# A selective scan with its last product on GpSimd and its step input in PSUM, and attention values on the whole TensorE array with their denominators as extra rows

## The chip, the cores and the metric

The kernel runs on one core of a Trainium2 chip. A core has TensorE (PE, matmuls into the accumulator memory PSUM), VectorE (DVE), ScalarE (ACT) and GpSimd (POOL), which work on the on-chip memory SBUF[...], and SyncE (SP), which issues DMA transfers. [...] Each engine runs its own instructions in order and waits for others by semaphores. The metric is the device time of one execution, in microseconds (us): the median of three runs is 20,853.4, the lowest 20,836.71, the highest 20,863.03.

## What is computed

The program is a chain of four layers on an input of 8 images, 64 channels (C), 64 x 64 pixels (L = 4096 positions). What matters here, from the reference:

```python
# layer 0: state-space scan, in four directions, 128 channels, 16 states
def step(h, inp):
    u_t, dt_t, B_t, C_t = inp
    h = h * jnp.exp(dt_t[..., None] * A) + dt_t[..., None] * B_t[:, :, None, :] * u_t[..., None]
    return (h, jnp.einsum('bkcn,bkn->bkc', h, C_t))
...
return jnp.moveaxis(ys, 0, -1) + D[None, :, :, None] * xs
...
# layer 1: position attention, q and k with 16 channels
energy_s = jnp.einsum('bon,bom->bnm', q, k)
att_s = jax.nn.softmax(energy_s, axis=-1)
out_s = jnp.einsum('bcn,bmn->bcm', v, att_s).reshape(b, c, h, w)
...
# layer 3: position attention, 64 channels
attention = jnp.einsum('nci,ncj->nij', xc, xb)
att = jax.nn.softmax(attention, axis=-1)
x_o = jnp.einsum('ncj,nij->nci', xd, att).reshape(n, c, h, w)
return alpha[0] * x_o + x
```

Before the scan stand a layer norm, a projection to 128 channels and a 3 x 3 depthwise convolution; after it a norm, a gate and a projection. Layer 0 ends with a gated convolution, layer 1 also has a channel attention, and layer 2 takes two training steps of a small network before it applies it. The change touches none of these.

## The kernel before

Three stages follow each other: `scan_layer` (to about 10,980 us of the span), `gate_and_attention` (the gated convolution, then the first attention, to about 14,900), and `modifier_and_attention` (the training steps, then the second attention from about 18,100 on).

**The scan.** For each of 8 images there are 16 chunks: four directions (in the order 0, 2, 1, 3) of four chunks of 1024 positions (CH). Each chunk runs over 16 states n, so there are 2048 inner steps. Channels lie on the 128 partitions, positions along the free dimension. One step:

- SP loads the rows n of B and of C, broadcast over all partitions, into the 1 MB tile `t` (L261; four buffers).
- ACT forms `a` = exp(dt A) (L263; two buffers).
- DVE multiplies `t[:,0]` by `du` in place (L264), scans `h` = a h + t0 along the chunk (L266) and multiplies `t[:,1]` by `h` in place (L271). The scan starts from the state column that the same n left in the chunk before.
- POOL copies the last column of `h` into the `state` tile (L270).
- PE adds `t[:,1]` into the PSUM tile `yps` by a matmul with the identity (L273).

After the 16 states a skip matmul (L279) adds D u, and `yps` goes into `y`: by an ACT copy for the first direction (L285), by a DVE add for the others (L287). `yps` has two buffers of two banks each; four banks are left for everything else.

`project` prepares the next chunk: matmul and ACT copy to `xd`, its rows B and C to memory (L233), a second matmul and ACT for `dt` (L236, L237), three ACT functions into `e` (L240 to L242), DVE's softplus sum `dt` (L243, two SBUF inputs) and POOL's `du` = dt u (L245). Directions 1 and 3 read u, and write y, across rows (`ordered`). At the end of an image `before(b+1)` (norm, projection, convolution L204) is issued before the last chunk's scan, and `after(b)` behind it: norm, then for each of eight blocks of 512 a matmul `zps`, ACT's gate, a DVE product (L304), the matmul `ops`, a DVE sum (L307). The order on each engine is set by the scheduler of the framework, from the order of the program and the buffers of the pools.

**The attentions** (`Attention.run`). For each image q, k and v are formed; v holds 32 blocks of 128 keys by 64 channels. The queries go in 8 blocks of 512. For each block 16 pairs of key blocks run through: scores on row tiles of the array (L426), an exp of 128 x 1024 on ACT (L431), sums of the exps on DVE (L436, L438), and values (L446). The values use two column tiles of the array: the even key block of a pair goes to partitions 0 to 63 of the PSUM tile `av`, the odd one to 64 to 127. The loop takes two pairs at a time (a group) and issues the scores of a group ahead of the values of the group before. Two groups after the end of a block comes `divide`: a matmul of the exp sums with a tile of ones (`sumps`, L454) spreads the denominators, DVE takes the reciprocal (L456), multiplies (L458) and records whether the denominators are in range (L462). Two groups later `finish` adds even and odd halves by a matmul with `fold` (the identity twice, one above the other). In the first attention it is added to the channel attention's matmul in the same PSUM tile and copied out by ACT (L744, L745, L747); in the second DVE adds the input (L1129, L1131).

Of the kernel before, what the change touches and what calls it, by code (L numbers as in the profile page):

```python
# [9 lines left out]
F32 = mybir.dt.float32  # L10
# [32 lines left out]
class Common:  # L43


    def __init__(self, ctx, tc):
        self.tc, self.nc = tc, tc.nc
        nc = self.nc
        self.open(ctx, "const")
        self.ident = self.tile([128, 128], "ident")  # L50
        make_identity(nc, self.ident)
        self.ones = self.tile([128, C], "ones")
        nc.vector.memset(self.ones, 1.0)
        self.all_ones = self.tile([128, 128], "all_ones")
        nc.vector.memset(self.all_ones, 1.0)

        self.fold = self.tile([128, C], "fold")
        nc.vector.tensor_tensor(self.fold, self.ident[:, :C], self.ident[:, C:], ALU.add)
# [75 lines left out]
def scan_layer(cm, x_in, w, xh):  # L134

    tc, nc = cm.tc, cm.nc
    with ExitStack() as ctx:
# [81 lines left out]
        def project(u, k, c):  # L219

            uo = ordered(u, k, c)
            half = BK // S
            xd = work.tile([R + 2 * N, CH], F32, name="xd", tag="xd")
            dt = work.tile([DI, CH], F32, name="dt", tag="dt")
            for i in range(CH // BK):
                ps = psum.tile([128, BK], F32, name="dps", tag="mm")
                nc.tensor.matmul(
                    ps[: R + 2 * N].rearrange("p (a b) -> p a b", b=S), wx[:, k, :],
                    uo[:, i * half : (i + 1) * half, :], start=True, stop=True,
                )  # L230
# [12 lines left out]
            nc.vector.scalar_tensor_tensor(dt, dt, 0.0, e, ALU.max, ALU.add)  # L243
            du = work.tile([DI, CH], F32, name="du", tag="du")
            nc.gpsimd.tensor_tensor(  # L245
                du.rearrange("p (a b) -> p a b", b=S), dt.rearrange("p (a b) -> p a b", b=S),
                uo, ALU.mult,
            )
            return dt, du, bc

        def scan(u, y, k, c, first, prep, state):
# [7 lines left out]
            for n in range(N):  # L259
                t = bcp.tile([DI, 2, CH], F32, name="t", tag="bc")  # L260
                nc.sync.dma_start(t, bcr[n].unsqueeze(0).broadcast_to([DI, 2, CH]))  # L261
                a = work.tile([DI, CH], F32, name="a", tag="a")
                nc.scalar.activation(a, dt, AF.Exp, scale=amat[:, k, n : n + 1])  # L263
                nc.vector.tensor_tensor(t[:, 0, :], t[:, 0, :], du, ALU.mult)  # L264
                h = work.tile([DI, CH], F32, name="h", tag="h")
                nc.vector.tensor_tensor_scan(  # L266
                    h[:, flip], a[:, flip], t[:, 0, flip],
                    0.0 if state is None else state[:, n : n + 1], ALU.mult, ALU.add,
                )
                nc.gpsimd.tensor_copy(new[:, n : n + 1], h[:, last : last + 1])  # L270
                nc.vector.tensor_tensor(t[:, 1, :], t[:, 1, :], h, ALU.mult)  # L271
                for i in range(CH // BK):
                    nc.tensor.matmul(  # L273
                        ps[:, bass.ts(i, BK)], cm.ident, t[:, 1, bass.ts(i, BK)],
# [83 lines left out]
class Attention:  # L358
# [3 lines left out]

    LOW, HIGH, VMAX = 1e-20, 1e26, 1e10

    def __init__(self, cm, ctx, name, d, qw, qb, kw, kb, vw, vb, gain, work, psum, sc, av):
# [19 lines left out]
        cm.load_t(work, psum, self.wv[:C, :], vw)  # L388
        nc.sync.dma_start(self.wv[C : C + 1, :], _row(vb))
        nc.vector.tensor_scalar(self.wv, self.wv, g, None, ALU.mult)  # L390

        self.lim = cm.tile([1, NB, NBK, 2], name + "_lim")
        self.vmax = cm.tile([128, NB], name + "_vmax")

    def run(self, b, xa, finish):
# [2 lines left out]
        cm, nc, d = self.cm, self.cm.nc, self.d  # L398
        q = self.pool.tile([128, L], F32, name="q", tag="q")
        k = self.pool.tile([128, L], F32, name="k", tag="k")  # L400
        v = self.pool.tile([128, TQ, C], F32, name="v", tag="v", bufs=2)
        for j in range(NBK):
            blk = bass.ts(j, BK)
            for t, wt in ((q, self.wq), (k, self.wk)):
# [8 lines left out]
            nc.vector.tensor_copy(v[:, 4 * j : 4 * j + 4, :], ps[:, :, :C])  # L413
        nc.vector.tensor_reduce(
            self.vmax[:, b : b + 1], v, AX.XY, ALU.max, apply_absolute_value=True
        )
        pairs = [(i, g) for i in range(NBK) for g in range(TQ // 2)]
        avs, sums, firsts = {}, {}, {}
        in_range = self.pool.tile([1, BK], F32, name="in_range", tag="in_range", bufs=1)

        def scores(i, g):
# [7 lines left out]
                )  # L429
            ex = self.exps.tile([128, 2, BK], F32, name="ex", tag="ex")  # L430
            nc.scalar.activation(ex, sc, AF.Exp)  # L431
            if g == 0:
                firsts[i] = ex
            elif g == 1:
                sums[i] = self.work.tile([128, 2, BK], F32, name="sum", tag="sum")
                nc.vector.tensor_tensor(sums[i], firsts[i], ex, ALU.add)  # L436
            else:
                nc.vector.tensor_tensor(sums[i], sums[i], ex, ALU.add)  # L438
            return ex

        def values(i, g, ex):
# [2 lines left out]
            av = avs[i]  # L444
            for e in range(2):
                nc.tensor.matmul(  # L446
                    av[e * C : (e + 1) * C, :], v[:, 2 * g + e, :], ex[:, e, :],
                    start=(g == 0), stop=(g == TQ // 2 - 1),
                )

        def divide(i):
            ps = self.psum.tile([128, BK], F32, name="sumps", tag="mm")
            for e in range(2):
                nc.tensor.matmul(ps, cm.all_ones, sums[i][:, e, :], start=(e == 0), stop=(e == 1))  # L454
            rr = self.work.tile([128, BK], F32, name="rr", tag="rr")
            nc.vector.reciprocal(rr, ps)  # L456
            o = self.work.tile([128, BK], F32, name="o", tag="o")
            nc.vector.tensor_tensor(o, rr, avs[i], ALU.mult)  # L458
            for e, (op, v0) in enumerate(
                ((ALU.is_ge, 1.0 / self.HIGH), (ALU.is_le, 1.0 / self.LOW))  # L460
            ):
                nc.vector.tensor_scalar(  # L462
                    in_range, rr[0:1, :], v0, None, op, ALU.min,
                    accum_out=self.lim[0:1, b, i, e : e + 1],
                )
            return o

        ahead, done = [], {}
        groups = [pairs[p : p + 2] for p in range(0, len(pairs), 2)]
        per = TQ // 4
        for n in range(len(groups) + 5):
            now = [(i, g, scores(i, g)) for i, g in groups[n]] if n < len(groups) else []
            for one in ahead:
                values(*one)
            ahead = now
            if n % per == 2 and n > per:
                done[n // per - 1] = divide(n // per - 1)  # L480
            if n % per == 4 and n > per:
                finish(n // per - 1, done.pop(n // per - 1))

    def out_of_range(self):

# [120 lines left out]
def gate_and_attention(cm, xh, w, a, x1, mixes, x2):  # L606

    tc, nc = cm.tc, cm.nc
    with ExitStack() as ctx:
# [56 lines left out]
        for b in range(NB):  # L666
# [416 lines left out]
def modifier_and_attention(cm, x2, w, a, x3, mixes, out):  # L1083
# [3 lines left out]
    with ExitStack() as ctx:  # L1087
# [25 lines left out]
        for b in range(NB):  # L1113
# [64 lines left out]
```

## Time and profile before

| what | value |
|---|---|
| median of three runs | 20,853.4 us |
| profiled execution | 20,863.03 us |
| its span | 20,861.2 us |
| mean granted TensorE clock | 0.772 of full speed |
| ACT, exp of the scan, L263 | 2,348.9 us in 2048 |
| POOL, state copy L270 / du L245 | 2,819.9 us in 2048 / 546.4 us in 128 |
| PE, identity matmuls L273 | 5,439.9 us in 8192 records |
| t loads | 2048 of 1,024 KB, median 5.3 us from issue to landing |
| DVE L456, reciprocal of 128 x 512 | mean 3.358 us |

The page gives for each group of instructions the busy time, the mean of one in ns, and the idle time of the engine ahead of it with what ended it. Line numbers are those of the kernel before. An fp32 matmul leaves two records, so the 2048 steps with two matmuls each give 8192. A chunk of the scan takes 76.6 us in the mean (twelve chunks from 1694.96 to 2614.26 us). DVE's longest single wait in the scan is 73.66 us at the end of an image, for `e`, which stands behind the convolution of the next image.

### The profile page before, as it was taken

The page shows a single profiled execution, that of the slowest core. Times are in us where ns is not written, and L with a number is a line of the kernel's source. Part 1 is how long each engine was busy: PE and PEld are TensorE (multiplying, and loading weights), DVE is VectorE, ACT ScalarE, POOL GpSimd, SP SyncE. Part 2 cuts the span into 40 slices and gives each one's busy share as a digit, 9 for nine tenths or more (in the row PEclk, how much of TensorE's full clock was granted, in tenths as well). Part 3 has the DMA queues.
Part 4 walks back from the last instruction along what each step waited for, and adds up shares of the span by engine and source line. Part 5 has one row for each costly group of instructions (what it writes and reads, how often), then busy time and mean ns, then how long its engine had stood idle before and what let it go on. Part 6 is the DMA issues. An engine that isn't in the chain of part 4 may idle for free. (4 is left out here: it accounts for less than half of the span.)

```text
span 20861.2 us, 120440 instructions
## 1 busy us (share of the span) xinstructions
PE 16934.2 (81%) x40899; PEld 5722.3 (27%) x40899; DVE 15083.2 (72%) x11926; ACT 7129.5 (34%) x7767; POOL 3525.7 (17%) x2316
## 2 busy tenths in 40 slices
PE   6676676766766767667668999999989989999999
PEld 2122222221211222222212222222234526333333
DVE  7989979899799798998993444444454726656656
ACT  3333333333333333433332223222313415333333
POOL 2332323323323232232230000000000000000000
PEclk8888787887888878878876777777765756788889
DMA  4646656566466565664660000000020100100000
GB/s 160 218 172 218 218 170 221 180 209 218 166 225 216 172 221 179 209 219 167 224 216 13 7 7 7 7 7 7 5 46 16 27 18 11 24 12 7 10 7 6
DMA packets 599802, 2315.54 MB, mean 111 GB/s; under 512 B 47480, under 2 KB 47752, under 8 KB 592520
## 3 DMA queue, kind: packets, MB, share of 16 engines
q1 hardware_dynamic: 599176, 2307.69, 33.2%
q8 instruction: 333, 5.46, 0.1%
q14 instruction: 293, 2.40, 0.0%
HBM read 2248.54 MB, written 58.98 MB: 111 GB/s over the span
## 5 line engine op out<-in xcount | busy, mean ns | idle before, releaser
L273 PE MATMUL yps<-t,ident 128*128 128x512 f32 x8192 | 5439.9, 801 | 3026.3 <-DVE t L271 2954.8
L263 ACT ACTIVATE a<-dt,amat 128x1024 f32<-128x1024 f32 x2048 | 2348.9, 1148 | 5972.5 <-DVE h L266 5970.5
L270 POOL COPY state<-h 128x1 f32<-128x1 f32 x2048 | 2819.9, 1378 | 6562.7 <-DVE h L266 6557.7
L266 DVE TENSOR_TENSOR_SCAN h<-a,state,t 128x1024 f32<-128x1024 f32 x1536 | 3612.0, 2353 | 12.6 <-ACT a L263 6.3
L273 PEld LDWEIGHTS yps<-t,ident 128*128 128x128 f32 x8192 | 1746.9, 235 | 6731.2 <-DVE t L271 4906.8
L431 ACT ACTIVATE ex<-sc 128x1024 f32<-128x1024 f32 x2048 | 1988.8, 1021 | 2518.8 <-PE sc L426 2518.8
L264 DVE TENSOR_TENSOR t<-t,du 128x1024 f32<-128x1024 f32 x2048 | 2706.5, 1323 | 45.6 <-DMA t<-bc 24.7
L438 DVE TENSOR_TENSOR sum<-sum,ex 128x1024 f32<-128x1024 f32 x1792 | 2184.6, 1219 | 661.2 <-ACT ex L431 570.9
L271 DVE TENSOR_TENSOR t<-t,h 128x1024 f32<-128x1024 f32 x2048 | 2480.8, 1213 | 1.9
L446 PE MATMUL av<-ex,v 128*64 128x512 f32 x8192 | 2009.2, 612 | 0.0
L426 PE MATMUL sc<-q,k 16*128 16x512 f32 (+1 forms) x8192 | 1799.0, 644 | 0.0
L639 PE MATMUL cvps<-pad,fw 64*64 64x512 f32 (+2 forms) x1728 | 1307.6, 959 | 56.1 <-DVE pad L682 56.1
L266 DVE TENSOR_TENSOR_SCAN h<-a,t 128x1024 f32<-128x1024 f32 x512 | 1166.2, 2280 | 3.6 <-ACT a L263 0.7
L426 PEld LDWEIGHTS sc<-q,k 16*128 16x128 f32 (+1 forms) x8192 | 595.3, 188 | 1055.3 <-ACT ex L431 607.7
L446 PEld LDWEIGHTS av<-ex,v 128*64 128x64 f32 x8192 | 503.3, 137 | 1363.1 <-issue 1348.3
L896 PE MATMUL yps<-a,w2T 128*64 128x512 f32 x640 | 575.6, 999 | 192.5 <-ACT a L889 192.4
L245 POOL TENSOR_TENSOR du<-dt,u 128x1024 f32<-128x1024 f32 x128 | 546.4, 4269 | 1038.1 <-DVE dt L243 1036.6
L660 DVE TENSOR_TENSOR gt<-cvps,dbl 64x512 f32<-64x512 f32 x64 | 43.7, 683 | 929.8 <-PE cvps L639 929.8
L704 POOL TENSOR_TENSOR gt<-gt,pad 64x512 f32<-64x512 f32 x64 | 75.2, 1175 | 3728.4 <-ACT gt L703 3590.8
L639 PEld LDWEIGHTS cvps<-pad,fw 64*64 64x64 f32 x1728 | 373.6, 226 | 990.2 <-issue 920.7
L243 DVE SCALAR_TENSOR_TENSOR dt<-dt,e 128x1024 f32<-128x1024 f32 x128 | 155.4, 1214 | 656.9 <-ACT e L242 656.8
L911 DVE BATCH_NORM_STATS2 yst<-yps 64x6 f32<-64x512 f32 x128 | 88.5, 691 | 697.3 <-PE yps L898 697.3
(321 smaller groups left out, 15027.4 us busy)
## 6 DMA issues: line engine op xcount, KB each, us to landing
t<-bc SPq DMA_DIRECT2D x2048, 1024.0 KB, 5.3
x<-x SPq DMA_DIRECT2D x80, 1024.0 KB, 7.4
bc<-xd SPq DMA_DIRECT2D x128, 128.0 KB, 3.4
xn<-in_x_dram SPq DMA_DIRECT2D x8, 1024.0 KB, 7.8
xr<-in_x_dram SPq DMA_DIRECT2D x64, 128.0 KB, 2.9
xh<-xr SPq DMA_DIRECT2D x64, 128.0 KB, 2.2
xt<-xh SPq DMA_DIRECT2D x8, 1024.0 KB, 9.6
x<-xa SPq DMA_DIRECT2D x8, 1024.0 KB, 6.8
```

The costliest lines, as they stand in the source:

```text
L263: nc.scalar.activation(a, dt, AF.Exp, scale=amat[:, k, n : n + 1])
L264: nc.vector.tensor_tensor(t[:, 0, :], t[:, 0, :], du, ALU.mult)
L266: nc.vector.tensor_tensor_scan(h[:, flip], a[:, flip], t[:, 0, flip], 0.0 if state is None else state[:, n : n + 1], ALU.mult, ALU.add,)
L270: nc.gpsimd.tensor_copy(new[:, n : n + 1], h[:, last : last + 1])
L271: nc.vector.tensor_tensor(t[:, 1, :], t[:, 1, :], h, ALU.mult)
L273: nc.tensor.matmul(ps[:, bass.ts(i, BK)], cm.ident, t[:, 1, bass.ts(i, BK)], start=(n == 0), stop=False,)
L426: nc.tensor.matmul(sc[:, e, :], k[rows, bass.ts(j, 128)], q[rows, bass.ts(i, BK)], start=True, stop=True,)
L431: nc.scalar.activation(ex, sc, AF.Exp)
L438: nc.vector.tensor_tensor(sums[i], sums[i], ex, ALU.add)
L446: nc.tensor.matmul(av[e * C : (e + 1) * C, :], v[:, 2 * g + e, :], ex[:, e, :], start=(g == 0), stop=(g == TQ // 2 - 1),)
L639: nc.tensor.matmul(ps, fw[:, i, t, :], pads[i][:, r0 + dy : r0 + nr + dy, dx : dx + n], start=(t == 0), stop=(t == 8),)
L896: nc.tensor.matmul(ps[:C], self.w2T, a, start=True, stop=not residual)
```

## The change

In the scan:

- `du` is formed by DVE into a PSUM tile (one buffer, two banks), not by POOL into SBUF.
- The product of B with `du` goes to a PSUM tile of its own, `z` (tag bdu, one buffer, two banks), and the scan reads it there; `t[:,0]` is left as loaded.
- The state column is copied by ACT, and the product of C with `h` is taken by POOL.
- `a` and `h` have three buffers, not two. `yps` has one, not two, and the pool for everything else two banks, not four; with them all eight banks are taken.

In the attentions:

- v is 128 wide: 64 channels of values and 64 columns of ones, in two tiles filled with ones once. One matmul on the whole array then gives the values in rows 0 to 63 of `av` and the denominators, 64 times, in rows 64 to 127. Even and odd key blocks add up in the same rows.
- The exp sums on DVE, `all_ones` with its matmul, and `fold` with its matmul are gone. The reciprocal, the product and `finish` follow directly behind the last values of a block; reciprocal and product cover 64 partitions. In both attentions `finish` is a DVE add into `o`, which is stored.

```diff
-        psum = ctx.enter_context(tc.tile_pool(name="s_psum", bufs=4, space=PSUM))
-        psy = ctx.enter_context(tc.tile_pool(name="s_psy", bufs=2, space=PSUM))
+        psum = ctx.enter_context(tc.tile_pool(name="s_psum", bufs=2, space=PSUM))
+        psy = ctx.enter_context(tc.tile_pool(name="s_psy", bufs=1, space=PSUM))
...
-            du = work.tile([DI, CH], F32, name="du", tag="du")
-            nc.gpsimd.tensor_tensor(
+            du = psy.tile([DI, CH], F32, name="du", tag="du")
+            nc.vector.tensor_tensor(
                 du.rearrange("p (a b) -> p a b", b=S), dt.rearrange("p (a b) -> p a b", b=S),
                 uo, ALU.mult,
             )
...
-                a = work.tile([DI, CH], F32, name="a", tag="a")
+                a = work.tile([DI, CH], F32, name="a", tag="a", bufs=3)
                 nc.scalar.activation(a, dt, AF.Exp, scale=amat[:, k, n : n + 1])
-                nc.vector.tensor_tensor(t[:, 0, :], t[:, 0, :], du, ALU.mult)
-                h = work.tile([DI, CH], F32, name="h", tag="h")
+                z = psy.tile([DI, CH], F32, name="bdu", tag="bdu")
+                nc.vector.tensor_tensor(z, t[:, 0, :], du, ALU.mult)
+                h = work.tile([DI, CH], F32, name="h", tag="h", bufs=3)
                 nc.vector.tensor_tensor_scan(
-                    h[:, flip], a[:, flip], t[:, 0, flip],
+                    h[:, flip], a[:, flip], z[:, flip],
                     0.0 if state is None else state[:, n : n + 1], ALU.mult, ALU.add,
                 )
-                nc.gpsimd.tensor_copy(new[:, n : n + 1], h[:, last : last + 1])
-                nc.vector.tensor_tensor(t[:, 1, :], t[:, 1, :], h, ALU.mult)
+                nc.scalar.copy(new[:, n : n + 1], h[:, last : last + 1])
+                nc.gpsimd.tensor_tensor(t[:, 1, :], t[:, 1, :], h, ALU.mult)
...
-        v = self.pool.tile([128, TQ, C], F32, name="v", tag="v", bufs=2)
+        v = self.v[b % 2]
...
-            if g == 0:
-                firsts[i] = ex
-            elif g == 1:
-                sums[i] = self.work.tile([128, 2, BK], F32, name="sum", tag="sum")
-                nc.vector.tensor_tensor(sums[i], firsts[i], ex, ALU.add)
-            else:
-                nc.vector.tensor_tensor(sums[i], sums[i], ex, ALU.add)
             return ex
...
                 nc.tensor.matmul(
-                    av[e * C : (e + 1) * C, :], v[:, 2 * g + e, :], ex[:, e, :],
-                    start=(g == 0), stop=(g == TQ // 2 - 1),
+                    av, v[:, 2 * g + e, :], ex[:, e, :],
+                    start=(g == 0 and e == 0), stop=(g == TQ // 2 - 1 and e == 1),
                 )
+            if g == TQ // 2 - 1:
+                blk = bass.ts(i, BK)
+                rr = self.work.tile([C, BK], F32, name="rr", tag="rr")
+                nc.vector.reciprocal(rr, av[C:, :])
+                o = self.work.tile([C, BK], F32, name="o", tag="o")
+                nc.vector.tensor_tensor(o, rr, av[:C, :], ALU.mult)
...
+                finish(i, o)
...
-                nc.tensor.matmul(ps[:C], cmapT, xa[:C, blk], start=True, stop=False)
-                nc.tensor.matmul(ps[:C], cm.fold, o, start=False, stop=True)
-                t = work.tile([C, BK], F32, name="x2t", tag="x2t")
-                nc.scalar.copy(t, ps[:C])
-                nc.sync.dma_start(x2[b][:, blk], t)
+                nc.tensor.matmul(ps[:C], cmapT, xa[:C, blk], start=True, stop=True)
+                nc.vector.tensor_tensor(o, o, ps[:C], ALU.add)
+                nc.sync.dma_start(x2[b][:, blk], o)
...
-                ps = psum.tile([128, BK], F32, name="fps", tag="mm")
-                nc.tensor.matmul(ps[:C], cm.fold, o, start=True, stop=True)
-                t = work.tile([C, BK], F32, name="outt", tag="outt")
-                nc.vector.tensor_tensor(t, ps[:C], x[:C, blk], ALU.add)
-                nc.sync.dma_start(ob[:, blk], t)
+                nc.vector.tensor_tensor(o, o, x[:C, blk], ALU.add)
+                nc.sync.dma_start(ob[:, blk], o)
```

More of the change, by code (lines that the diff above doesn't have):

```diff
@@ L53, in __init__ @@
         nc.vector.memset(self.ones, 1.0)
[L54 to L58, printed above, removed]
         self.spread = self.tile([NBK, NBK, 128], "spread")
@@ L390, in __init__ @@
         nc.vector.tensor_scalar(self.wv, self.wv, g, None, ALU.mult)
+        self.v = []
+        for i in range(2):
+            v = self.pool.tile([128, TQ, 128], F32, name=f"v{i}", tag=f"v{i}")
+            nc.gpsimd.memset(v[:, :, C:], 1.0)
+            self.v.append(v)
         self.lim = cm.tile([1, NB, NBK, 2], name + "_lim")
@@ L412, in run @@
                 )
-            nc.vector.tensor_copy(v[:, 4 * j : 4 * j + 4, :], ps[:, :, :C])
+            nc.vector.tensor_copy(v[:, 4 * j : 4 * j + 4, :C], ps[:, :, :C])
         nc.vector.tensor_reduce(
-            self.vmax[:, b : b + 1], v, AX.XY, ALU.max, apply_absolute_value=True
+            self.vmax[:, b : b + 1], v[:, :, :C], AX.XY, ALU.max, apply_absolute_value=True
         )
         pairs = [(i, g) for i in range(NBK) for g in range(TQ // 2)]
-        avs, sums, firsts = {}, {}, {}
+        avs = {}
         in_range = self.pool.tile([1, BK], F32, name="in_range", tag="in_range", bufs=1)
@@ L446, in values @@
                 nc.tensor.matmul(
-                    av[e * C : (e + 1) * C, :], v[:, 2 * g + e, :], ex[:, e, :],
-                    start=(g == 0), stop=(g == TQ // 2 - 1),
-                )
[L451 to L475, printed above, removed]
+                    av, v[:, 2 * g + e, :], ex[:, e, :],
+                    start=(g == 0 and e == 0), stop=(g == TQ // 2 - 1 and e == 1),
+                )
+            if g == TQ // 2 - 1:
[4 more added lines that the diff above has]
+                nc.vector.tensor_tensor(o, rr, av[:C, :], ALU.mult)
+                for e, (op, v0) in enumerate(
+                    ((ALU.is_ge, 1.0 / self.HIGH), (ALU.is_le, 1.0 / self.LOW))
+                ):
+                    nc.vector.tensor_scalar(
+                        in_range, rr[0:1, :], v0, None, op, ALU.min,
+                        accum_out=self.lim[0:1, b, i, e : e + 1],
+                    )
+                finish(i, o)
+        ahead = []
+        for p in range(0, len(pairs), 2):
+            now = [(i, g, scores(i, g)) for i, g in pairs[p : p + 2]]
             for one in ahead:
@@ L478, in run @@
             ahead = now
[L479 to L482, printed above, removed]
+        for one in ahead:
+            values(*one)
     def out_of_range(self):
```

## The prediction, written before the changed kernel had run

> **What bounds the kernel now.** I read the page's busy shares and its 40 slices first, then the groups, then busy time by window, and last the timeline of one inner step in each stage.
>
> ```profile
> PE 16934.2 (81%) x40899; PEld 5722.3 (27%) x40899; DVE 15083.2 (72%) x11926; ACT 7129.5 (34%) x7767; POOL 3525.7 (17%) x2316
> PE   6676676766766767667668999999989989999999
> DVE  7989979899799798998993444444454726656656
> ...
> L266 DVE TENSOR_TENSOR_SCAN h<-a,state,t 128x1024 f32<-128x1024 f32 x1536 | 3612.0, 2353 | 12.6 <-ACT a L263 6.3
> L264 DVE TENSOR_TENSOR t<-t,du 128x1024 f32<-128x1024 f32 x2048 | 2706.5, 1323 | 45.6 <-DMA t<-bc 24.7
> L438 DVE TENSOR_TENSOR sum<-sum,ex 128x1024 f32<-128x1024 f32 x1792 | 2184.6, 1219 | 661.2 <-ACT ex L431 570.9
> L271 DVE TENSOR_TENSOR t<-t,h 128x1024 f32<-128x1024 f32 x2048 | 2480.8, 1213 | 1.9
> L446 PE MATMUL av<-ex,v 128*64 128x512 f32 x8192 | 2009.2, 612 | 0.0
> ```
>
> The overall 81% of PE misleads: the slices split at the 21st. Up to about 10,950 us (the scan layer) DVE is full; behind it PE is. The windows say it of the steady parts (columns: PE, PEld, DVE, ACT, POOL busy, clock, DMA share, GB/s):
>
> ```profile
> 1500.00:5000.00 3500.00, 2450.34 (x3830) 756.29 (x3829) 3257.47 (x2162) 1278.66 (x1289) 1076.04 (x706) 0.80 0.59 203
> 12000.00:12100.00 100.00, 100.00 (x480) 29.06 (x474) 83.31 (x78) 55.96 (x60) 0.00 (x0) 1.00 0.03 6
> ```
>
> So the two halves of the change act on two different limits: in the scan a cut in DVE work pays one for one; in the attentions added PE work costs one for one, and the DVE sums that go (L438) are worth nothing.
>
> One inner step of the scan (DVE) and three cases of dependence and sharing:
>
> ```profile
> 1796.22 2.34 DVE L266 TENSOR_TENSOR_SCAN h<-a,state,t 128x1024 f32<-128x1024 f32 x1
> 1798.48 1.20 DVE L264 TENSOR_TENSOR t<-t,du 128x1024 f32<-128x1024 f32 x1
> 1799.60 1.21 DVE L271 TENSOR_TENSOR t<-t,h 128x1024 f32<-128x1024 f32 x1
> 1800.73 2.34 DVE L266 TENSOR_TENSOR_SCAN h<-a,state,t 128x1024 f32<-128x1024 f32 x1
> 1800.87 1.98 PE L273 MATMUL yps<-t,ident 128*128 128x512 f32 x4 [1.05 <-DVE t L271]
> ...
> 1438.54 1.23 DVE L264 TENSOR_TENSOR t<-t,du 128x1024 f32<-128x1024 f32 x1
> 1438.69 3.27 POOL L245 TENSOR_TENSOR du<-dt,u 128x1024 f32<-128x1024 f32 x1 [74.99 <-DVE dt L243]
> 1439.87 4.24 DVE L266 TENSOR_TENSOR_SCAN h<-a,state,t 128x1024 f32<-128x1024 f32 x1
> 1446.60 2.35 DVE L266 TENSOR_TENSOR_SCAN h<-a,state,t 128x1024 f32<-128x1024 f32 x1
> 1448.99 1.22 DVE L271 TENSOR_TENSOR t<-t,h 128x1024 f32<-128x1024 f32 x1
> ...
> 5002.02 2.24 POOL L270 COPY state<-h 128x1 f32<-128x1 f32 x1 [2.28 <-DVE h L266]
> ```
>
> Pitch 4.51 us (1796.22 to 1800.73). Because the program alternates independent operations, each starts 0.08 us before the one ahead ends. Where an operation needs the one just ahead of it, it starts later than that one's end: product to scan +0.10 (1438.54+1.23 to 1439.87; up to 0.13 elsewhere, 0.11 used below), scan to product +0.04 (1446.60+2.35 to 1448.99). And POOL and DVE hold each other up: a scan takes 4.24 us beside the POOL product, and a 128x1 copy on POOL takes 2.24 us.
>
> Attention, one group of two key pairs:
>
> ```profile
> 12004.59 1.14 PE L426 MATMUL sc<-q,k 16*128 16x512 f32 x8
> ...
> 12005.66 1.94 PE L446 MATMUL av<-ex,v 128*64 128x512 f32 x8
> ```
>
> Eight value records on two column tiles take 1.94 us; four records on the full array (L273 above) 1.98.
>
> [...] The trace agrees (8 records in 1.94 against 4 in 1.98 us), so giving it up doubles the values' time. [...] The trace's shortest L245 is 2.34, and that is used. [...] L458 with a PSUM input has a mean of 676 ns, L970 from SBUF alone 682.
>
> **Attention, part by part.** Full-array records on the identity follow each other 0.43 to 0.48 us apart (1.98 for four, 7.13 for sixteen in a row); eight value records then take about 3.63 us to the next start instead of 1.87. A block of eight groups takes 28.28 us in the first attention now (from one sumps to the next: 8 x 3.05, sumps 1.91, two fps about 2.0) and then 8 x (1.06 + 3.63) + 1.0 = 38.5: +10.2. In the second, with scores of 1.92, it goes from 33.1 to 8 x (1.92 + 3.63) = 44.4: +11.3. There are 64 blocks each: 64 x 21.5 = +1,376. DVE's sums, ACT's copy L747 and the reciprocal's half size lie beside PE and are worth nothing; ScalarE's two exps (2.04) fit in 4.69. At the 16 batch ends PE waits 2.45 us for a reciprocal before the last fps, and runs on values alone while the divide is under way; this goes: -70 taken (0 to -110). Sum **+1,306**.
>
> **Scan, per inner step.** Removed from DVE: the product with h. Left: z = t0*du, scan. There is one z buffer, so z(n+1) needs scan(n) done and scan(n+1) needs z(n+1): both gaps are now the dependent kind. 1.22 + 0.11 + 2.35 + 0.04 = **3.72 us** (4.51 before). Bounds: [...] the gaps may be as small as between independent operations (-0.08 each: 3.41). POOL's product (2.34) runs beside the next z and scan[...]; ScalarE's exp 1.15 and a small copy fit twice over. New waits: the state copy on ScalarE waits for h, and behind it in that queue stand only exps, which run up to three steps ahead (a has three buffers); the state itself is wanted a whole chunk later, so the copies cost nothing unless ScalarE falls a step behind. On POOL nothing but products is left; on SP each t load still waits for its buffer's last matmul. I take 3.72 because both gaps are measured.
>
> **Scan, per chunk.** Fifteen steps, 55.8. At the seam DVE runs z(15) 1.26; dt (L243 of before, two SBUF inputs) which waits for the POOL product that began with z(15), 1.1 (0 to 2.3); itself 1.13; du, moved here from POOL, 1.5 (1.2, or up to 2.35 where u is read across rows); scan(15) 2.39. Sum 63.2. The y-add behind the second scan of the next chunk: 1.21 for one direction, 2.33 for two, none for the first, mean 1.5. With one yps buffer the next chunk's first matmul waits for that add, and t's release with it: t(0) is free about 11 us into the chunk, its reload lands 5.3 us later at 16.3, wanted at about 16.4. So 0 to 4; I take 2. Chunk 66.7 against 76.6 (1694.96 to 2614.26 over twelve L243): -9.9 x 128 = -1,267. What hides POOL's product is the scan of the next step; at the batch ends that cover is gone, and the gate chain with one buffer slot less (zps behind the previous ops) stands bare where it was interleaved with scans: +15 for each of 8, +120 (0 to 200). The 74 us wait for the convolution at each end stays. Sum **-1,147**.
>
> Together +159 on the profiled execution of 20,863.0 (span 20,861.2); that stands 10 above the median, 20,853.4. On the median: about **21,012 us**.
>
> **Rivals.** A is that sum. **B, the buffers bind.** A t buffer's round is DMA 5.3, z and scan 3.7, POOL 2.34, PE 1.98 (3.46 at half clock, as at 1796.36), 0.3 of hand-overs: 13.6 to 15.1 us against 4 x 3.72 = 14.9, and the DMA share would go from 0.59 to 0.71. For it: PE will idle more in each step[...], and landings reach 9.8 us. Against: L264 now waits only 24.7 us in all for DMA. A pitch of 3.95 gives 2048 x 0.23 = +470: 21,480. **C, not slower.** The gaps between dependent DVE operations shrink, because z goes to PSUM and scan reads it there, and the seam's 2 us don't occur. It decides below a pitch of 3.65 (159 / 2048 = 0.08 less). With 3.5 and 1.5 us a seam saved: -450 - 190, about 20,370; with 3.55 alone 20,660. Against it: the gaps measured above. **D, the lock holds even with a PSUM operand.** Then z, product and scan run in turn, 1.26 + 2.34 + 2.39 = 6.0: 2048 x 2.28 = +4,670, about 25,700. [...]
>
> **How the numbers follow.** A 0.48, B 0.26, C 0.21, D 0.05. The forecast is A's. Its own range is 20,750 to 21,270; for 8 in 10 I reach to 20,560 (much of C) and 21,520 (most of B), leaving out C's far end and D. A difference of 0.2% (42 us) is about what a measurement of this kernel can tell. A gives 0.03 faster, 0.06 same, 0.39 slower; B and D 0.31 slower; C 0.18 faster, 0.02 same, 0.01 slower. Faster 0.21, same 0.08, slower 0.71.
>
> **What would show it.** The value matmuls: eight in 3.6 us, PE full in both attentions, blocks of 38.5 and 44.4. The scan: starts 3.72 apart, POOL at 2.34 and not 4, L243's successor waiting about 1 us on POOL, chunks of 66.7, the stage's end near 9,830 instead of 10,980. B shows as DVE waiting for DMA at z; D as POOL products in between z and scan. It is wrong if the pitch leaves 3.6 to 3.85, or if value matmuls cost less than 3.4 us a group.

## The result: 21,101 us, 1.2% slower, and the profile after

The changed kernel takes 21,101.51 us (median of four, 21,078.12 to 21,163.37) against 20,854.67 for the kernel before (four runs). The ratio is 1.0124, with an interval of 1.0102 to 1.0147. The forecast was 21,012. The profiled execution has a span of 21,095.2 us against 20,861.2: +234.

From the page after: the busy line, a row of the slices, and the groups (busy time, mean ns, idle time ahead and what ended it).

```profile
PE 17499.9 (83%) x40131; PEld 6361.4 (30%) x40131; DVE 10879.6 (52%) x8148; ACT 7203.9 (34%) x9681; POOL 4997.0 (24%) x2192
...
PE   6676766767676676766999999999899999999999
...
L269 POOL TENSOR_TENSOR t<-t,h 128x1024 f32<-128x1024 f32 x2048 | 4824.7, 2356 | 5074.9 <-DVE h L264 4494.9
L441 PE MATMUL av<-ex,v 128*128 128x512 f32 x8192 | 3809.9, 608 | 0.0
L264 DVE TENSOR_TENSOR_SCAN h<-a,state,bdu 128x1024 f32<-128x1024 f32 x1536 | 3602.4, 2345 | 188.9 <-ACT a L260 3.6
L262 DVE TENSOR_TENSOR bdu<-t,du 128x1024 f32<-128x1024 f32 x2048 | 2514.1, 1228 | 376.6 <-DMA t<-bc 320.5
L268 ACT COPY state<-h 128x1 f32<-128x1 f32 x2048 | 389.7, 190 | 4765.2 <-DVE h L264 4755.6
```

DVE has lost 4,200 us of work and the kernel is slower. The scan's operations have kept their durations (scan 2.345 us against 2.353, and POOL's product 2.356, though the two run side by side), while `av` has gone from 2,009 to 3,810 us of PE. New in the list is the 320 us that z waits for the loads of t, where L264 of before waited 24.7.

The stages say where the time went. The last gate sum of the scan stage starts at 10,006.6 us, against 11,057.8 before: **-1,051**. The rest follows by subtraction: 234 + 1,051 = +1,285. Not all of that is the attentions' doing. The windows reach from the first score of each attention to its last reciprocal, with the training steps between the two (columns as in the prediction); before first, then after:

```profile
11324.70:15230.20 3905.50, 3714.65 (x11973) 1155.33 (x11973) 1824.44 (x1815) 1211.03 (x1353) 136.20 (x112) 0.74 0.03 6
15230.20:18031.80 2801.60, 2556.86 (x6949) 1200.77 (x6949) 1426.60 (x1650) 923.82 (x1325) 0.00 (x0) 0.61 0.12 26
18031.80:20848.50 2816.70, 2746.50 (x9543) 911.74 (x9542) 1707.17 (x1659) 1045.93 (x1094) 0.00 (x0) 0.87 0.04 8
```

```profile
10275.80:14867.60 4591.80, 4394.70 (x11591) 1550.79 (x11591) 713.35 (x917) 1174.30 (x1290) 136.05 (x112) 0.77 0.02 5
14867.60:17576.70 2709.10, 2458.25 (x6946) 1143.28 (x6946) 1425.83 (x1651) 920.79 (x1324) 3.56 (x2) 0.63 0.12 27
17576.70:21080.30 3503.60, 3447.27 (x9161) 1339.05 (x9160) 557.34 (x700) 1045.46 (x1094) 0.00 (x0) 0.91 0.03 6
```

The attentions lose 686 and 687, together **+1,373**. The training steps, which the change does not touch, took 92 us less in this one execution, at a granted clock of 0.63 where it was 0.61. In the traces of the other kernels below this stretch takes from 2,703 to 2,872 us, so the 92 is scatter between executions.

The inner step after, in the timeline (start, duration, engine and line, idle time ahead):

```profile
1796.61 1.23 DVE L262 TENSOR_TENSOR bdu<-t,du 128x1024 f32<-128x1024 f32 x1
1796.70 2.35 POOL L269 TENSOR_TENSOR t<-t,h 128x1024 f32<-128x1024 f32 x1 [1.39 <-DVE h L264]
1797.97 2.35 DVE L264 TENSOR_TENSOR_SCAN h<-a,state,bdu 128x1024 f32<-128x1024 f32 x1
1799.11 1.98 PE L271 MATMUL yps<-t,ident 128*128 128x512 f32 x4 [1.76 <-POOL t L269]
1800.35 1.23 DVE L262 TENSOR_TENSOR bdu<-t,du 128x1024 f32<-128x1024 f32 x1
1801.71 2.35 DVE L264 TENSOR_TENSOR_SCAN h<-a,state,bdu 128x1024 f32<-128x1024 f32 x1
```

The pitch is 3.74 us (1796.61 to 1800.35) where it was 4.51. z to scan leaves 0.13 us (1796.61 + 1.23 to 1797.97), scan to z 0.03. POOL's product lies beside both.

The attentions' blocks, read from the reciprocals (one for each block), on DVE's timeline in the first and the second attention:

```profile
11008.90 3.36 DVE L448 RECIPROCAL rr<-av 64x512 f32<-64x512 f32 x1 [32.73 <-PE av L441]
11047.51 3.36 DVE L448 RECIPROCAL rr<-av 64x512 f32<-64x512 f32 x1 [32.73 <-PE av L441]
...
17710.82 3.36 DVE L448 RECIPROCAL rr<-av 64x512 f32<-64x512 f32 x1 [38.51 <-PE av L441]
17755.21 3.36 DVE L448 RECIPROCAL rr<-av 64x512 f32<-64x512 f32 x1 [38.50 <-PE av L441]
```

A block takes 38.61 us in the first and 44.39 in the second. DVE waits for PE for 32.73 and 38.50 of it: the work taken from DVE was taken from an engine that waits.

The seam between two chunks of a direction that writes y across rows (these lines are from the timeline of all engines):

```profile
2163.47 3.78 PE L271 MATMUL yps<-t,ident 128*128 128x512 f32 x4 [3.74 <-POOL t L269]
2167.04 3.62 PE L277 MATMUL yps<-u,skipd 128*128 128x512 f32 x4
2170.70 2.32 DVE L285 TENSOR_TENSOR y<-y,yps 128x1024 f32<-128x1024 f32 x1 [2.32 <-PE yps L277]
2172.93 1.22 DVE L262 TENSOR_TENSOR bdu<-t,du 128x1024 f32<-128x1024 f32 x1
2173.12 3.60 PE L271 MATMUL yps<-t,ident 128*128 128x512 f32 x4 [2.46 <-issue]
...
2183.11 1.23 DVE L262 TENSOR_TENSOR bdu<-t,du 128x1024 f32<-128x1024 f32 x1 [2.74 <-DMA t<-bc]
```

Read it downwards. PE has stood idle for 3.74 us and takes 3.78 us for the last product, which takes 1.98 in the inner step above (at a granted clock of 1.00), then 3.62 for the skip. The two are slow for different reasons, as two windows and a line of PE show (the first window lies on this last product, the second on the projection for the next chunk, which also reads u across rows):

```profile
2163.50:2167.00 3.50, 3.50 (x4) 1.48 (x5) 3.33 (x3) 1.24 (x2) 2.23 (x1) 0.50 0.00 1
2150.20:2153.70 3.50, 3.50 (x5) 0.40 (x4) 3.33 (x3) 3.07 (x4) 2.13 (x2) 1.00 0.86 279
2150.20 3.60 PE L222 MATMUL dps<-u,wx 128*36 128x512 f32 x4
```

The last product ran at a granted clock of 0.50. Four records that read u across rows take 3.60 us even at 1.00; the skip's records have a mean of 1.04 us across rows (1.03 in the kernel before) and of 0.73 in row order (0.60 before). DVE stands 2.32 us for it ahead of the y add, which takes 2.32 itself. Until that add is done the next chunk's matmuls can't enter `yps`, its one buffer, so they start at 2173.12. They are what gives t's buffers back; ten microseconds later z waits 2.74 us for a load.

### The profile page after: what moved, and what is told of

Its sections match the earlier page's. It is cut to its first block, busy times and chain, and to the rows that moved or that the text cites. A ratio compares the mean times of both kernels' runs of the same rounds, so it can differ in the third digit from the quotient of the medians.

```text
span 21095.2 us, 117073 instructions
## 1 busy us (share of the span) xinstructions
PE 17499.9 (83%) x40131; PEld 6361.4 (30%) x40131; DVE 10879.6 (52%) x8148; ACT 7203.9 (34%) x9681; POOL 4997.0 (24%) x2192
## 5 line engine op out<-in xcount | busy, mean ns | idle before, releaser
L271 PE MATMUL yps<-t,ident 128*128 128x512 f32 x8192 | 4756.7, 713 | 2797.5 <-POOL t L269 2634.3
L269 POOL TENSOR_TENSOR t<-t,h 128x1024 f32<-128x1024 f32 x2048 | 4824.7, 2356 | 5074.9 <-DVE h L264 4494.9
L441 PE MATMUL av<-ex,v 128*128 128x512 f32 x8192 | 3809.9, 608 | 0.0
L264 DVE TENSOR_TENSOR_SCAN h<-a,state,bdu 128x1024 f32<-128x1024 f32 x1536 | 3602.4, 2345 | 188.9 <-ACT a L260 3.6
L271 PEld LDWEIGHTS yps<-t,ident 128*128 128x128 f32 x8192 | 1610.2, 216 | 5952.1 <-POOL t L269 4191.0
L448 DVE RECIPROCAL rr<-av 64x512 f32<-64x512 f32 x128 | 430.0, 3359 | 4606.8 <-PE av L441 4606.8
L262 DVE TENSOR_TENSOR bdu<-t,du 128x1024 f32<-128x1024 f32 x2048 | 2514.1, 1228 | 376.6 <-DMA t<-bc 320.5
L441 PEld LDWEIGHTS av<-ex,v 128*128 128x128 f32 x8192 | 1483.0, 191 | 2268.5 <-issue 2268.5
L268 ACT COPY state<-h 128x1 f32<-128x1 f32 x2048 | 389.7, 190 | 4765.2 <-DVE h L264 4755.6
L264 DVE TENSOR_TENSOR_SCAN h<-a,bdu 128x1024 f32<-128x1024 f32 x512 | 1170.3, 2286 | 61.3 <-ACT a L260 1.7
L238 DVE SCALAR_TENSOR_TENSOR dt<-dt,e 128x1024 f32<-128x1024 f32 x128 | 229.5, 1793 | 702.4 <-ACT e L237 698.2
L872 PE MATMUL hnps<-x,hw 65*128 65x512 f32 x640 | 544.7, 947 | 15.0 <-DVE x L1103 15.0
```

Of the source, the lines that this page charges most:

```text
L262: nc.vector.tensor_tensor(z, t[:, 0, :], du, ALU.mult)
L264: nc.vector.tensor_tensor_scan(h[:, flip], a[:, flip], z[:, flip], 0.0 if state is None else state[:, n : n + 1], ALU.mult, ALU.add,)
L269: nc.gpsimd.tensor_tensor(t[:, 1, :], t[:, 1, :], h, ALU.mult)
L271: nc.tensor.matmul(ps[:, bass.ts(i, BK)], cm.ident, t[:, 1, bass.ts(i, BK)], start=(n == 0), stop=False,)
L441: nc.tensor.matmul(av, v[:, 2 * g + e, :], ex[:, e, :], start=(g == 0 and e == 0), stop=(g == TQ // 2 - 1 and e == 1),)
L448: nc.vector.reciprocal(rr, av[C:, :])
```

## The experiments

Each was timed beside the kernel before on the same chip. Its medians there were 20,797.3 us (the two halves, the values without ones, z in SBUF), 20,798.0 (two z buffers, loads apart, y summed by PE, both edits) and 20,767.9 (the state copy on POOL and the two shifts of buffers at the end). A ratio is to these, with its interval. Where there was one run, only the difference is given.

**The attention half alone.** The scan is that of before, the rest that of after.

> The attention half of the change alone, the scan as before. Theory (two stages, two limits, no interplay): the blocks grow from 28.3 to 38.6 and from 33.05 to 44.4 us, 128 blocks, less the batch ends: +1,285, so 22,140 us (22,100 to 22,180). Rival (part of the loss comes from elsewhere, for instance from a scan stage that gained less than its trace says): between 21,500 and 22,000.

22,169 us, ratio 1.0665 (1.0633 to 1.0697): +1,372, which is what the windows give (1,373). The +1,285 by subtraction, on which the expectation rests, would be 6.2%, a little under the interval: it had the shorter training steps in it. The rival is out.

**The scan half alone.**

> The scan half alone, the attentions as before. Theory: the last gate sum of the scan stage falls 1,051 us earlier, and nothing behind it changes: 19,800 us (19,760 to 19,850). Rival (the scan's gain is partly eaten by the later stages, or borrowed from them): above 19,900.

19,708 us, ratio 0.9470 (0.9442 to 0.9498): -1,090. That is below the range expected, which was worked out from 20,854 us, 57 more than the kernel before took on this chip; the rest, 39 us, is within the interval. The two halves add: 6.65% less 5.30% is 1.35%, and the change gave 1.24%. So the change is a gain of 5.3% and a loss of 6.7% in one.

**The values without the columns of ones** (on the attention half alone). The denominators are left out: the reciprocal reads the ones of v instead, and a clamp stands in place of the product.

```diff
-                    av, v[:, 2 * g + e, :], ex[:, e, :],
+                    av[:C, :], v[:, 2 * g + e, :C], ex[:, e, :],
```

> The attention half alone, with the value matmuls cut to the 64 columns of values: no columns of ones, still all key blocks into the same 64 rows. The denominators are left out; the output block is the clamped sum. Theory (what costs is that two key blocks no longer share the array as two column tiles): the same as with the ones, blocks of 38.6 and 44.4 us, 22,140. Rival (the 64 columns of ones are what is paid for): values back at 1.9 us a group, blocks near 26 and 32, 20,600 to 20,900.

22,142 us in one run, 27 less than with the ones. The groups of the two kernels, with ones first:

```profile
L438 PE MATMUL av<-ex,v 128*128 128x512 f32 x8192 | 3810.0, 608 | 0.0
```

```profile
L438 PE MATMUL av<-ex,v 128*64 128x512 f32 x8192 | 3764.6, 603 | 2.3 <-DVE o L447 2.3
```

By these means a matmul of 64 columns costs nearly what one of 128 does. A block takes 38.19 and 43.96 us (medians, from one end of the value matmuls to the next), where with the ones it takes 38.61 and 44.39: the ones cost about 1% of a block. What costs is that two key blocks no longer run side by side as column tiles. The blocks show this better than the totals, since in this run the training steps happened to take 132 us more than with the ones. In the kernel before the same 64-column records stand at 2,009 us for the same count.

**z in SBUF** (on the scan half alone). The product with du goes back into t.

```diff
-                z = psy.tile([DI, CH], F32, name="bdu", tag="bdu")
+                z = t[:, 0, :]
```

> As the scan half alone, but the product with du goes back in place into SBUF, so that the scan has two SBUF inputs again (a and z), beside the POOL product. Theory[...]: scan and POOL product run in turn, so the pitch goes from 3.74 to about 6.0 us, 2048 x 2.27 = +4,600: near 24,400. Rival (POOL does not hinder DVE here, PSUM only saved nothing): pitch 3.7 to 3.9, 19,800 to 20,100.

21,098 us in one run: +1,390 to the scan half alone, less than a third of what I expected, and not the rival either. Its timeline:

```profile
2006.07 1.19 DVE L267 TENSOR_TENSOR t<-t,du 128x1024 f32<-128x1024 f32 x1
2006.28 2.36 POOL L274 TENSOR_TENSOR t<-t,h 128x1024 f32<-128x1024 f32 x1 [2.28 <-issue]
2007.39 3.39 DVE L269 TENSOR_TENSOR_SCAN h<-a,state,t 128x1024 f32<-128x1024 f32 x1
...
2010.71 1.19 DVE L267 TENSOR_TENSOR t<-t,du 128x1024 f32<-128x1024 f32 x1
```

The pitch is 4.64 us. The scan, with two SBUF inputs, is held up beside POOL's product: it takes 3.39 us instead of 2.35. It ends 2.14 us after POOL's product, which ends at 2008.64, as if it had got going only then. But z, with du still in PSUM, has one SBUF input and runs beside the product at 1.19 us, so only product and scan come in turn: POOL works 2.36 us and idles 2.28, the 4.64, and not 6.0. My sum had z in the row as well. The operand in PSUM is worth 0.9 us a step (4.64 less 3.74), and with z in SBUF the scan half would not beat the kernel before.

**The state copy back on POOL** (on the scan half alone).

```diff
-                nc.scalar.copy(new[:, n : n + 1], h[:, last : last + 1])
+                nc.gpsimd.tensor_copy(new[:, n : n + 1], h[:, last : last + 1])
```

> The scan half alone, with one part undone: the state column is copied by POOL again, in front of the product. Theory (each POOL copy costs about 1.1 us in POOL's queue, and POOL then needs 1.1 + 2.35 = 3.45 of the 3.74 us pitch): the product ends later in each step, t and h are held 1.1 us longer, the pitch stays near 3.74 in quiet stretches and the seams lose 1 to 3 us: 19,707 + 128 x 2 = 19,960 (19,750 to 20,200). Rival (a POOL copy of one column takes 1.4 us or more here, so POOL becomes the bound): pitch 3.8 to 4.0, 20,000 to 20,400.

19,817 us, ratio 0.9530 (0.9488 to 0.9572). The interval overlaps that of the scan half (0.9442 to 0.9498), so a cost of about 110 us is likely and not certain. It lies in the range expected, but the reason given was wrong, as the groups show:

```profile
L274 POOL TENSOR_TENSOR t<-t,h 128x1024 f32<-128x1024 f32 x2048 | 4822.6, 2355 | 3.5 <-POOL state L273 3.5
L273 POOL COPY state<-h 128x1 f32<-128x1 f32 x2048 | 382.2, 187 | 4839.7 <-DVE h L269 4740.8
```

The copy takes 0.187 us, not 1.1. Most of the cost shows at z, which waits 349.3 us for loads of t where it was 279.2 in the scan half alone; the rest is open. In the kernel before the same copy took 1.378 in the mean, with DVE at work on two SBUF inputs in every step:

```profile
1798.48 1.20 DVE L264 TENSOR_TENSOR t<-t,du 128x1024 f32<-128x1024 f32 x1
1798.62 1.10 POOL L270 COPY state<-h 128x1 f32<-128x1 f32 x1 [3.41 <-DVE h L266]
```

This copy ends at 1799.72, 0.04 us behind the end of DVE's product. The two kernels differ in more than this, so that the difference is a wait for DVE is inferred, and from the scan with z in SBUF likely.

**Two z buffers, each scan issued behind the next z** (on the scan half alone). To make room in PSUM, y is summed into one bank and du is formed for half of the chunk and used twice, so y is not the layer's.

```diff
-                z = psy.tile([DI, CH], F32, name="bdu", tag="bdu")
+                    z = psy.tile([DI, CH], F32, name="bdu", tag="bdu", bufs=2)
...
+                with tc.issue_after(zi.ins):
+                    nc.vector.tensor_tensor_scan(
```

> The scan half alone, with two z buffers and each scan issued behind the z of the next state. To make room in PSUM, yps is one bank into which both halves of the chunk are summed, and du is formed for the first half of the chunk alone and used for both halves, so y is not the layer's y. Theory (a DVE operation that needs the one just ahead starts 0.13 us after its end, an independent one 0.08 ahead of it): z to scan saves 0.2 us, scan to z stays dependent at 0.04 since z's buffer was read by that scan: pitch 3.74 to 3.54. Rival (the gap belongs to the PSUM write or read, whoever made it): pitch stays 3.7.

21,281 us in one run: 1,573 slower than the scan half alone. Where all buffers were free, the step did shorten. From its timeline, and its z group on all of the scan:

```profile
2000.19 1.23 DVE L269 TENSOR_TENSOR bdu<-t,du 128x1024 f32<-128x1024 f32 x1
2001.33 2.28 DVE L280 TENSOR_TENSOR_SCAN h<-a,bdu 128x1024 f32<-128x1024 f32 x1
2003.65 1.23 DVE L269 TENSOR_TENSOR bdu<-t,du 128x1024 f32<-128x1024 f32 x1
```

```profile
L269 DVE TENSOR_TENSOR bdu<-t,du 128x1024 f32<-128x1024 f32 x2048 | 2513.8, 1227 | 2516.0 <-DMA t<-bc 2483.7 <-DVE h L280 0.7
```

The scan starts 0.09 us ahead of z's end and z 0.04 after the scan's: 3.46 us with a scan of 2.28, that is 3.53 with one of 2.35, as expected. So the gap ahead of the scan is one of dependence, not of PSUM: this scan reads z from PSUM as well, and the gap of 0.13 us is gone. That the kernel as a whole would be slower was not forecast: DVE waits 2,484 us for t loads. The likely reason is that z(n+1), formed one scan earlier, holds its 1 MB t one scan longer, which is what the forecast's rival B describes. It is argued, not shown, since y is also formed in another way here and two z buffers were not tried with the loads apart.

**B and C loaded apart** (on the scan half alone). Instead of four buffers for both rows, three for B and five for C, of half the size.

```diff
-                t = bcp.tile([DI, 2, CH], F32, name="t", tag="bc")
-                nc.sync.dma_start(t, bcr[n].unsqueeze(0).broadcast_to([DI, 2, CH]))
+                tb = bcp.tile([DI, CH], F32, name="tb", tag="tb", bufs=3)
+                nc.sync.dma_start(tb, bc[n : n + 1, :].broadcast_to([DI, CH]))
+                t = bcp.tile([DI, CH], F32, name="t", tag="tc", bufs=5)
+                nc.sync.dma_start(t, bc[N + n : N + n + 1, :].broadcast_to([DI, CH]))
```

> The scan half alone, with the 1 MB tile t cut in two of 0.5 MB with a load each: the rows of B in three buffers, free again as soon as z is formed, the rows of C in five. The memory used stays the same. Theory (the wait for t loads behind the seam comes from buffers that are held until the identity matmul): DVE's wait for DMA at z, 320 us in the changed kernel, falls below 100; 19,800 - 250 = 19,550 (19,480 to 19,650). Rival (the loads are late because the DMA engines are too busy, or the second load's issue costs): waits as before or more, 19,780 to 19,950.

19,349 us, ratio 0.9310 (0.9286 to 0.9334): -358 to the scan half alone, more than expected. The z groups of the scan half alone and of this kernel, and its scan:

```profile
L267 DVE TENSOR_TENSOR bdu<-t,du 128x1024 f32<-128x1024 f32 x2048 | 2514.5, 1228 | 335.0 <-DMA t<-bc 279.2
```

```profile
L268 DVE TENSOR_TENSOR bdu<-tb,du 128x1024 f32<-128x1024 f32 x2048 | 2513.8, 1227 | 64.5
L270 DVE TENSOR_TENSOR_SCAN h<-a,state,bdu 128x1024 f32<-128x1024 f32 x1536 | 3602.6, 2345 | 559.6 <-POOL t L275 362.9
```

The 279 us for DMA are gone. The B half of a tile is used up by z, yet it was held until PE had added the C half. The amount of data is the same, and the DMA engines moved it faster: 232 and 236 GB/s at a share of 0.68 and 0.69 (1500 to 5000 us, 5000 to 9500), against 224 and 225 at 0.65 in the changed kernel. So the loads had been late for want of a free buffer, not of bandwidth. The 363 us that scans wait for POOL are seven waits of 52 us, one at the end of each image but the last. They stand in place of DVE's wait of 67 us for `e` at L243, whose group waited 697 us in the scan half alone and 226 here. So some 280 of the 358 us are the late loads, and most of the rest is won at the ends of images, for a reason that was not tried by itself.

**y summed by PE, copied out by ACT** (on the scan half alone).

```diff
-            if first:
-                nc.scalar.copy(yo, pv)
-            else:
-                nc.vector.tensor_tensor(yo, yo, pv, ALU.add)
+            if not first:
+                for i in range(CH // BK):
+                    nc.tensor.matmul(
+                        ps[:, bass.ts(i, BK)].rearrange("p (a b) -> p a b", b=S), cm.ident,
+                        yo[:, i * half : (i + 1) * half, :], start=False, stop=True,
+                    )
+            nc.scalar.copy(yo, pv)
```

> The scan half alone, with the y sum taken off DVE: PE adds y into yps by an identity matmul (y read as it lies), and ACT copies yps into y for all four directions. Theory (the seam is DVE's y add, 1.96 us in the mean, its wait for PE, 1.7, and the t loads that are late behind it): 96 seams x 3.7 = -355 less some 60 for yps being held longer: 19,500 (19,420 to 19,620). Rival (yps with one buffer is the limit, and PE's two more matmuls and ACT's place in its queue hold it longer than DVE did): 19,750 to 20,000.

19,991 us, ratio 0.9620 (0.9593 to 0.9646): the rival held, and it is 284 us slower than the scan half alone.

```profile
L267 DVE TENSOR_TENSOR bdu<-t,du 128x1024 f32<-128x1024 f32 x2048 | 2515.2, 1228 | 960.1 <-DMA t<-bc 902.5
```

DVE has 96 adds less, 189 us, and their wait for PE, 160 us, is gone with them; but z waits 902 us for loads instead of 279. What t's buffers hang on is how long `yps` stays taken: from the end of a chunk's last scan to the first matmul of the next chunk it is 15.4 us in the mean across rows, against 11.9 in the scan half alone.

**Both edits together.**

> Both edits together: split loads of B and C, y summed by PE and copied by ACT. Theory: they answer to the same seam, so the sum is less than both: 19,350 (19,250 to 19,480). Rival (independent, they add): below 19,250; or they compete for one wait: no better than the better one.

19,209 us, ratio 0.9226 (0.9200 to 0.9251). That is less than the 19,250 to 19,480 expected. The expectation had taken both edits for gains; in fact the one that cost 284 us with the shared tile gains 140 with the loads apart. This points to t, held while `yps` was taken, as the source of the loss, and speaks against what PE and ACT had more to do.

**The buffers shifted once more**, on both edits: B with two buffers, and h with four, or C with six.

> As both edits together (split loads, y summed by PE), with two buffers for the rows of B instead of three, and four for h instead of three. Theory (what is left between the measured chunk and fifteen pitches is scans that wait for an h buffer, held by POOL's product): the chunks of the two directions that write y across rows fall from 65.6 to 63.5 us: 19,100 (19,020 to 19,180). Rival (the load of B is late with two buffers): z waits for DMA, 19,250 to 19,500.

> As both edits together, with two buffers for the rows of B and six for the rows of C. Theory (the rows of C are still held too long at the seam, since yps has one buffer): POOL's wait for DMA falls, 19,100 (19,020 to 19,180). Rival (as above, the load of B is late): 19,250 to 19,500. If both this and the run with four h buffers come out alike and slower, two buffers for B are too few.

Four h: 19,217 us, ratio 0.9243 (0.9203 to 0.9282), no difference to both edits: neither the gain expected nor the rival's loss. Six for C: 19,124 us, ratio 0.9180 (0.9140 to 0.9219), in the range expected; its interval overlaps that of both edits, so a gain of about 0.5% is likely and not certain. It does not come from where it was expected: POOL's wait for DMA goes from 485 only to 465 us, while z's wait for the rows of B goes from 96 to 12. Two buffers for B are enough: with four h, z waits 100. This version, with the attentions of before, beats both kernels: by 8.2% the one before, and by 9.3% the changed one (0.9180 / 1.0124 = 0.907).

## Why the prediction was right, point by point

**The two limits: right.** Two halves measured alone, +6.65% and -5.30%, add to the measured 1.24% within their intervals.

**The sum: right, and close in part by luck.** Forecast were +1,306 and -1,147, together +159. The stages give +1,373 and -1,051, together +322: both terms missed to the same side, by 67 and 96. In the two profiled executions the training steps gave 92 of this back by chance, which leaves about the +234. The medians differ by 247, the two halves timed alone give 282.

**Attention, per block: right.** 38.5 and 44.4 us were forecast, 38.61 and 44.39 measured. The working, doubling of the value records, is shown by the run without ones. 64 x (10.33 + 11.34) = 1,387, and the windows give 1,373, so the batch ends gave back 14 by the two traces, where 70 were taken. That is nearly all of the 67 by which the attentions cost more than forecast.

**The pitch: right.** 3.72 forecast, 3.74 measured, from gaps of 0.13 and 0.03. Rival C needed 3.65 or less; the run with two z buffers shows that dependence alone costs 0.2 us a step. There 3.53 was reached only where the loads were in time, which with four shared t buffers they mostly were not.

**The PSUM operand beside POOL's product: right.** That z and scan, with one SBUF input each, would run beside the product was the author's assumption: the lines of before that the forecast shows have only a scan with two, of 4.24 us. In the changed kernel the scan with z in PSUM takes 2.345 us in the mean, z 1.228 and POOL's product 2.356, and the timeline above has them side by side; in the run with z in SBUF the scan takes 3.39. Rival D, with z, product and scan in turn at 6.0 us, did not occur; where product and scan alone came in turn the pitch was 4.64.

**The PSUM price: small, as in the trace of before.** z with one PSUM input and a PSUM output takes 1.228 us against 1.213 for L271 between SBUF tiles (1.195 is the median of L264), and the scan 2.345 against 2.353: at most 0.033 us an operation.

**The seam: the term that was too small.** Forecast was a chunk of 66.7 us. Measured from one L238 to another, twelve chunks from 1552.31 to 2371.08 us take 68.2. Of these, the chunks of the directions that keep the row order take 64.9 to 66.9, those across rows 69.2 to 72.9. The y adds on DVE, before and after:

```profile
L287 DVE TENSOR_TENSOR y<-y,yps 128x1024 f32<-128x1024 f32 x96 | 188.7, 1966 | 33.1 <-PE yps L279 32.9
```

```profile
L285 DVE TENSOR_TENSOR y<-y,yps 128x1024 f32<-128x1024 f32 x96 | 188.6, 1965 | 165.0 <-PE yps L277 165.0
```

The adds come to 188.6 / 128 = 1.5 us a chunk, as taken, and the late loads to 320.5 / 128 = 2.5 where 2 were taken: the prediction had that chain (yps, matmul, t's release, load), and its middle value was near (most, 3.9 a chunk, are behind the first direction, where ACT copies `yps`). It put at nothing DVE's wait for PE ahead of the add, 165.0 / 128 = 1.3 us a chunk and 2.1 in the mean across rows, where the slow skip stands ahead of it. The run with loads apart brings the chunks across rows to 67.4 to 68.3, both edits to 63.6 to 67.5 (read in the same way). 1.5 us x 128 = 192 of gain are missing. (The forecast's stage end of 10,980 is the last y add, which starts at 10,971.6; after, it starts at 9,910.0, where 9,830 was forecast.)

**The batch end: the term that was too large.** From one of the long waits at L238 to the next, a batch takes 1236.1 us after (1306.46 to 2542.60), 1365.5 before (1437.31 to 2802.81). Less sixteen chunks, 145 against 140 remain: +5 a batch where +15 was taken, and +1 in the mean of six images (1232.7 and 1366.5 us), so 80 to 110 us of loss are missing. Of the two errors 80 to 110 us remain, which covers the 96 between -1,147 and -1,051. Why the bare gate chain cost so little was not tried by itself.

## What to carry to other kernels

Price each part of a change against the engine that bounds its own stage: here one stage's 5.3% gain was hidden by the other's 6.7% loss, and taking DVE work out of a stage that PE bounds brought nothing (DVE waits for PE for 32.73 of the 38.61 us of a block). When a step gets shorter, count how long each of its buffers is held and by which last reader; a tile that joins two inputs with different last readers is held for the later one, and loading them apart was worth 358 us, some 280 of it in late loads, with no byte more of memory. Two small matrices side by side as column tiles halved the time of the matmuls that need 64 columns (2,009 us against 3,765), and 64 columns more on the untiled ones cost almost nothing (3,810): that is one choice, not two savings.

## What the runs showed of the hardware that was not expected

A POOL copy of one column takes 0.187 us in the mean in the run with the copy back on POOL, where z and scan have one SBUF input each, and took 1.378 in the kernel before, where DVE worked on two: a small operation that lasts long on POOL may be waiting, not working. Such a wait can be seen in a duration, not only in idle time: the scan's record is 3.39 us long with z in SBUF, and 2.35 with z in PSUM. The time of four matmul records went from 1.98 us (granted clock 1.00) to 3.78 where the granted clock was 0.50, and to 3.60 at 1.00 where PE read its input across rows. In the trace of the changed kernel the first kind of slowness comes and goes with the clock, the second does not: the skip's records in row order have a median of 0.592 us where their own granted clock is 0.95 or more and of 1.061 where it is below 0.55, those across rows 1.033 and 1.061. And a wait can outweigh the operations that stood ahead of it: 96 y adds taken off the bound engine made the kernel 284 us slower.
